# A read of the third gather back, ahead of each gather of an image's first six chunks

## The chip, the core and the metric

The kernel runs on one core of a Trainium2 chip. A core has five engines with their own instruction streams: TensorE (PE, matrix products and transposes), VectorE (DVE), ScalarE (ACT), GpSimd (POOL) and SyncE (SP, which here only starts transfers). Sixteen DMA engines move data between the chip's memory (HBM) and the core's own (SBUF). The metric is the device time of one launch in microseconds. The three runs of the kernel before gave 4634.28, 4643.66 and 4647.31 us, so the median is 4643.66 us.

## What is computed

The input is eight images of 256 channels and 64 x 64 pixels, all in f32. Two layers follow each other, each adding to its input. The first is a local attention of 3 x 3 pixels with a generated convolution kernel. The second, which the change is about, is a deformable 3 x 3 convolution: from the normed image a small convolution finds, for each pixel and each of nine taps, where to sample; four neighbouring pixels are read there, weighted, summed, and multiplied with the convolution's weights.

```python
# layer 0: group norm, 3x3 local attention, projection
x = x + _L0_conv_ref(_gn(x), w_qkv, w_kg, b_kg, alpha, beta, w_proj)
# layer 1: group norm, modulated deformable 3x3 convolution
x = x + _L1_conv_ref(_gn(x), w_off, b_off, w)
...
# in layer 1, with y0, x0, ly, lx from the offsets, for 9 taps and 64x64 pixels:
v = samp(y0, x0) * (1 - ly) * (1 - lx) + samp(y0, x0 + 1) * (1 - ly) * lx \
  + samp(y0 + 1, x0) * ly * (1 - lx) + samp(y0 + 1, x0 + 1) * ly * lx
return jnp.einsum('bckhw,ock->bohw', v * mask, w)
```

## The kernel before

**Two halves side by side.** An image is worked in eight chunks of 512 pixels. The "front" is the whole first layer and the preparation of the second: attention, norm, a table of the normed image in HBM, and the sampling places (`idx`) and weights (`wt`). The other half is the deformable convolution itself. While image b is convolved, the front of image b + 1 runs: `fronts()` is a generator that does one step at a time, and the main loop takes a step after each half slot. The last image is convolved without any front beside it. All four compute engines run their instructions in the order in which this program writes them down.

**The convolution.** A slot is one tap of one chunk: 72 slots an image, four blocks of 128 pixels in each, so 288 blocks an image and 2304 in all. A block goes through these lines:

- `gather` (line 1037): GpSimd issues an indirect DMA that reads, for each of 128 pixels, 4 KB from the table (all four corners, 256 channels each) into a buffer `g` of 128 x 1024 f32, 512 KB. There are ten such buffers (`GATHERS = 10`).
- `scale` (line 1053): ACT writes the first corner, times its weight, to `s`.
- `sum_corners` (line 1061): DVE adds the other three corners, each with its weight; three instructions a block, six in a row for a pair of blocks.
- `transposes` (line 1091): TensorE turns the four blocks' `s`; ACT copies the result to `vt` (line 1094).
- `product` (line 1116): TensorE multiplies with the weights, eight matmuls a slot, into `po`.

**What runs how far ahead.** At block i the loop scales blocks i + 8 and i + 9, sums blocks i + 6 and i + 7, then takes a step of the front, and then calls `gathers(i)`, which issues the gathers of blocks i + 16 and i + 17 (`LEAD = 16`). Their buffers are those of blocks i + 6 and i + 7, so they wait for the sums that were just put down. The DMAs of GpSimd go round eight semaphores ("lanes"): a gather waits for the landing of the gather eight before it, for DVE and for ACT.

**What else stands on GpSimd.** `gathers` first writes one element of a tile that TensorE is to have read (`holds`, the memset of line 1077), 223 times in all: the gathers behind it wait until TensorE is there. In the last image a memset of 128 x 160 (line 1082) follows each gather. In images 0 to 6 nothing stands between the two gathers of a pair.

**Other transfers.** SP starts loads of the next image's chunks, writes the table, stores the first layer's result (`kept`) and the output, and loads `r`, the first layer's result, back: 196 MB beside the gathers' 1208 MB. Loads of the next image stand mostly in the second half of an image's convolution.

The functions that the change touches, and what calls them:

Of the kernel before, what the change touches and what calls it, by code (L numbers as in the profile page):

```python
# [9 lines left out]
F32 = mybir.dt.float32  # L10
# [7 lines left out]
P = 128  # L18
# [7 lines left out]
NB = N // P  # L26
NC = H // R
KK = 9
# [17 lines left out]
BLOCKS = SLOTS * NB  # L46
# [3 lines left out]
LEAD = SUM_AHEAD + GATHERS  # L50
# [7 lines left out]
def preact_kernel(ctx: ExitStack, tc: tile.TileContext, a: dict, out: bass.AP):  # L58
# [17 lines left out]
    nc = tc.nc  # L76
# [3 lines left out]
    const = ctx.enter_context(tc.tile_pool(name="const", bufs=1))  # L80
# [74 lines left out]
    for i in range(min(2, B)):  # L155
# [7 lines left out]
        for o in range(H * WP, ENTRIES, P):  # L163
            n = min(P, ENTRIES - o)
# [862 lines left out]
    holds: list = []  # L1027
    rest = const.tile([P, 1], F32, name="rest")
    pause = const.tile([P, 160], F32, name="pause")

    def gather(i):
        if i >= B * BLOCKS:
            return
        b, n = divmod(i, BLOCKS)
        c, k, j = n // NB // KK, n // NB % KK, n % NB
        g = gp.tile([P, 4 * C], F32, tag="g", name=f"g_{i}")
        nc.gpsimd.indirect_dma_start(  # L1037
            out=g,
            out_offset=None,
            in_=tables[b % 2],  # L1040
            in_offset=bass.IndirectOffsetOnAxis(ap=found[b, c][0][:, j, k : k + 1], axis=1),
        )
        rows[i] = g
# [30 lines left out]
    def gathers(i):  # L1074

        if holds:
            nc.gpsimd.memset(holds.pop(), 0.0)
        last = i + LEAD >= (B - 1) * BLOCKS
        for n in range(2):
            gather(i + LEAD + n)  # L1080
            if last:
                nc.gpsimd.memset(pause, 0.0)
# [65 lines left out]
    with tc.manual_schedule(engines=ordered):  # L1148
# [24 lines left out]
        last = None  # L1173
        for n in range(B * SLOTS + 1):
            late, last = last, None
            if n > 0 and n % KK == 0:
                last = divmod(n // KK - 1, NC)
            for m in range(NT):
                if n < B * SLOTS:
                    if m == 0:  # L1180
                        transposes(*divmod(n, SLOTS))
                    if not last:
                        ahead(NB * n + 2 * m)
                if late and m == 0:
                    stored(*late)
                if n > 0:
                    product(*divmod(n - 1, SLOTS), m)
                if last:

                    finished(*last, m)  # L1190
                    ahead(NB * n + 2 * m)
                    if n == B * SLOTS:
                        stored(*last, slice(m, m + 1))

                h = NT * n + m + 1
                goal = h * STEPS + min(h, STEPS) * (STEPS_AHEAD - STEPS_FIRST)
                while (done - STEPS - STEPS_FIRST) * STEPS < goal:
                    state["quiet"] = next(steps, True)
                    done += 1
                if n < B * SLOTS:  # L1200
                    gathers(NB * n + 2 * m)
# [76 lines left out]
```

## Time and profile before

| | |
|---|---|
| median of three runs | 4643.66 us |
| the profiled execution | 4625.93 us |
| its span, first to last instruction | 4624.2 us |
| TensorE's granted clock, mean over the span | 0.992 |
| bytes moved | 1412.46 MB, 305 GB/s in the mean |
| gathers, all issued by GpSimd | 2304, 73.9% of the DMA engines' time |
| transfers started by SP and ACT | 11.7% of the DMA engines' time |

The profile is of one execution. "Busy" is the time in which an engine executes; time in which an instruction stands and waits is not in it. For each group of instructions the profile gives the busy time, the mean of one in ns, and the idle time of the engine just before them, with what ended that idle time: the engine or transfer whose signal came last. The chain of waits follows the work that ended last back through the span, and shares the span out among those that held it up. An indirect DMA shows as two things: the instruction on GpSimd, which writes the transfer's descriptors, and the transfer itself, whose packets and whose sixteen updates of its lane's semaphore are recorded too, not all of the updates.

Images 0 to 6 take about 555 us each. Within one, a chunk's 36 gathers take 65 to 70 us in chunks 0 to 5 and about 75 in chunk 6.

### The profile page before, as it was taken

Reading aid. Unit: us, or ns where it says so; the run is one execution under the profiler, and the core shown is the slowest. Engines: PE = TensorE matmul, PEld = TensorE weight load, DVE = VectorE, ACT = ScalarE, POOL = GpSimd, SP = SyncE. Lnnn points to the kernel's source line nnn. Section 1 sums busy time; section 2 is a strip of 40 time slices with the busy share of each in tenths; the row PEclk is TensorE's granted clock in tenths of the full one; section 3 lists DMA queues with packets and bytes.
Section 4 is the critical chain, followed back from the end, with each engine's and each line's share of the span. In section 5 each row is a group of like instructions: output and inputs, shape, how many; then the busy total and the mean of one; then the engine's idle time right before and its main releaser. Section 6 shows DMA issues by size and latency. Waiting matters only on the chain.

```text
span 4624.2 us, 77590 instructions
## 1 busy us (share of the span) xinstructions
PE 4486.9 (97%) x25344; PEld 2327.6 (50%) x25344; DVE 4132.8 (89%) x10183; ACT 2522.0 (55%) x5283; POOL 2685.1 (58%) x2840
## 2 busy tenths in 40 slices
PE   8989999999999999999999999999999999998888
PEld 4445555555545555455554555555555555543443
DVE  5669999999999999999998999999999999987887
ACT  3345556555565555655555555555556555554554
POOL 0035655566556655556655666555655656568887
PEclk9989999999999999999999999999999999999999
DMA  3078889988998888988899888998889988898998
GB/s 106 24 246 297 305 307 354 323 293 297 316 373 303 295 311 310 382 300 295 311 320 359 299 305 303 340 346 300 304 315 360 322 290 293 301 343 323 363 362 321
DMA packets 445761, 1412.46 MB, mean 305 GB/s; under 512 B 46430, under 2 KB 63070, under 8 KB 445228
## 3 DMA queue, kind: packets, MB, share of 16 engines
q0 software_dynamic: 331776, 1208.11, 73.9%
q1 hardware_dynamic: 111564, 196.04, 11.7%
q8 instruction: 199, 3.26, 0.3%
q10 hardware_dynamic: 2016, 3.36, 0.2%
q14 instruction: 206, 1.69, 0.1%
HBM read 1275.97 MB, written 131.36 MB: 304 GB/s over the span
## 4 chain that ended last, share of the span: by engine, by line
PE 84%; DMA 5%; DVE 5%; issue 2%; POOL 2%; ACT 2%; another core or an unknown queue 1%; SPq 0%; POOLq 0%; ACTq 0%; DVEq 0%
PE po L1116 37%; PE pt L1091 10%; PE psk L345 5%; PE proj L590 5%; PE psv L345 5%; PE psq L314 5%; PE om L817 4%; DMA g<-table,idx 3%; DVE s L1061 3%; PE av L577 3%; PE vk L559 2%; PE qk L388 2%; PE wk L536 2%; PE gen L431 1%; POOL g L1037 1%
## 5 line engine op out<-in xcount | busy, mean ns | idle before, releaser
L1037 POOL DMA_INDIRECT g<-table,idx x2304 | 2582.2, 1121 | 1702.6 <-issue 537.8
L1061 DVE SCALAR_TENSOR_TENSOR s<-g,wt,s 128x256 f32<-128x256 f32 x6912 | 2825.0, 477 | 162.2 <-ACT s L1053 124.3
L1116 PE MATMUL po<-vt,w_conv 128*128 128x512 f32 x4608 | 2192.0, 601 | 1.0 <-issue 1.0
L1116 PEld LDWEIGHTS po<-vt,w_conv 128*128 128x128 f32 x4608 | 810.8, 191 | 772.3 <-issue 763.2
L1053 ACT ACTIVATE s<-g,wt 128x256 f32<-128x256 f32 x2304 | 1058.6, 511 | 256.9 <-DMA g<-table,idx 187.5
L1094 ACT COPY vt<-pt 128x512 f32<-128x512 f32 x1152 | 617.3, 589 | 394.0 <-PE pt L1091 311.8
L1091 PE MATMUL pt<-ident,s 128*128 128x128 f32 x4608 | 648.0, 279 | 55.8 <-ACT vt L1094 21.6
L1091 PEld LDWEIGHTS pt<-ident,s 128*128 128x128 f32 x4608 | 522.2, 142 | 332.8 <-issue 173.6
L817 PE MATMUL om<-xn,w_off 128*32 128x512 f32 (+1 forms) x2560 | 273.8, 555 | 0.6 <-DVE xn L264 0.6
L345 PE MATMUL psv<-xn,w_qkvT 128*128 128x512 f32 (+1 forms) x576 | 248.9, 559 | 0.0
L345 PE MATMUL psk<-xn,w_qkvT 128*128 128x512 f32 (+1 forms) x576 | 246.9, 558 | 0.0
L314 PE MATMUL psq<-xn,w_qkvT 128*128 128x512 f32 x512 | 242.8, 605 | 3.9 <-issue 3.4
L590 PE MATMUL proj<-acc,w_projT 128*128 128x512 f32 x512 | 239.5, 593 | 0.7 <-ACT acc L584 0.7
L401 DVE TENSOR_TENSOR qk<-qk,near_k 128x400 f32<-128x400 f32 x256 | 134.7, 567 | 95.6 <-PE qk L388 55.9
L322 ACT COPY q<-psq 128x512 f32<-128x512 f32 x128 | 74.9, 585 | 235.8 <-PE psq L314 229.4
L584 ACT COPY acc<-av 128x512 f32<-128x512 f32 x128 | 74.8, 584 | 216.8 <-PE pt L1091 140.7
L356 ACT COPY k<-psk 128x512 f32<-128x512 f32 (+1 forms) x144 | 78.8, 551 | 201.8 <-PE psk L345 182.4
L577 PEld LDWEIGHTS av<-wk,vk 100*64 100x64 f32 x4096 | 132.2, 137 | 101.6 <-issue 49.7
L817 PEld LDWEIGHTS om<-xn,w_off 128*32 128x32 f32 x2560 | 75.6, 109 | 208.4 <-issue 201.1
L564 ACT COPY vk<-vk 100x512 f32<-100x512 f32 x256 | 139.1, 592 | 72.6 <-PE vk L559 62.3
L544 DVE TENSOR_TENSOR wk<-wk,near 100x512 f32<-100x512 f32 x256 | 158.6, 680 | 12.7 <-PE wk L536 12.7
L345 PEld LDWEIGHTS psk<-xn,w_qkvT 128*128 128x128 f32 x576 | 104.4, 190 | 122.6 <-issue 109.7
(104 smaller groups left out, 3440.3 us busy)
## 6 DMA issues: line engine op xcount, KB each, us to landing
table<-ts SPq DMA_DIRECT2D x128, 384.0 KB
g<-table,idx POOLq DMA_INDIRECT x2304
x<-in_x_dram SPq DMA_DIRECT2D x61, 512.0 KB
x<-x SPq DMA_DIRECT2D x56, 512.0 KB
r<-x SPq DMA_DIRECT2D x56, 512.0 KB
out_dram<-r SPq DMA_DIRECT2D x56, 512.0 KB
table<-ts SPq DMA_DIRECT2D x128, 128.0 KB
out_dram<-y SPq DMA_DIRECT2D x7, 512.0 KB
```

The source lines that it names most:

```text
L314: nc.tensor.matmul(ps, w_qkvT[:, ct, m * P : (m + 1) * P], window(self.xn, ct, 4), start=(ct == 0), stop=(ct == NT - 1),)
L345: nc.tensor.matmul(ps[:, : (hi - lo) * W], w_qkvT[:, ct, o : o + P], self.xn[:, ct, lo:hi, 1 : W + 1], start=(ct == 0), stop=(ct == NT - 1),)
L544: nc.vector.tensor_mul(wk.rearrange("p (t n) -> p t n", n=T * T), ps[:NK].rearrange("p (t n) -> p t n", n=T * T), near.unsqueeze(1).to_bro ...
L577: nc.tensor.matmul(av[64 * h : 64 * h + 64, g, t * T * T : (t + 1) * T * T], self.vk[:, t, o : o + 64], self.wk[2 * g + h][:, i * n + t * ...
L590: nc.tensor.matmul(ps, w_projT[:, ct, m * P : (m + 1) * P], self.acc[:, ct].rearrange("p (t y x) -> p y t x", y=T, x=T), start=(ct == 0), ...
L817: nc.tensor.matmul(self.ps[32 * g : 32 * g + 32, cols], w_off[:, ct, k, :], window(self.xn, ct, k)[:, ys], start=(n < 4), stop=(tail >= 0),)
L1037: nc.gpsimd.indirect_dma_start(out=g, out_offset=None, in_=tables[b % 2], in_offset=bass.IndirectOffsetOnAxis(ap=found[b, c][0][:, j, k : ...
L1053: nc.scalar.activation(s, g[:, 0:C], AF.Copy, scale=w[:, 0:1])
L1061: nc.vector.scalar_tensor_tensor(s, g[:, q * C : (q + 1) * C], w[:, q : q + 1], s, ALU.mult, ALU.add)
L1091: nc.tensor.transpose(pt[ct][:, j, :], s[:, ct * P : (ct + 1) * P], ident)
L1094: nc.scalar.copy(v[:, ct, :], pt[ct].rearrange("p b n -> p (b n)"))
L1116: nc.tensor.matmul(po[m], w_conv[:, ct, k, m * P : (m + 1) * P], v[:, ct, :], start=(k == 0 and ct == 0), stop=(b + 1 < B and k == KK - 1 ...
```

## The change

Ahead of each of the two gathers, GpSimd copies one element per partition (128 x 1) of the buffer of the gather that stands three ahead of it in the order of gathers into a new tile `landed`, which nothing reads. A copy must wait until the buffer that it reads has landed. It is done while `i % 288 < 216`, that is while the first six chunks of an image are convolved, and not once gathers of the last image are issued. Since gathers run 16 blocks ahead, these are the 17th to the 232nd gather of each of images 0 to 6: 216 x 7 = 1512 copies.

```diff
@@ -1027,6 +1027,7 @@
     holds: list = []
     rest = const.tile([P, 1], F32, name="rest")
     pause = const.tile([P, 160], F32, name="pause")
+    landed = const.tile([P, 1], F32, name="landed")
 
     def gather(i):
         if i >= B * BLOCKS:
@@ -1077,6 +1078,8 @@
             nc.gpsimd.memset(holds.pop(), 0.0)
         last = i + LEAD >= (B - 1) * BLOCKS
         for n in range(2):
+            if i % BLOCKS < (NC - 2) * KK * NB and not last:
+                nc.gpsimd.tensor_copy(landed, rows[i + LEAD + n - 3][:, 0:1])
             gather(i + LEAD + n)
             if last:
                 nc.gpsimd.memset(pause, 0.0)
```

In the program as built, each copy waits for the lane of the gather three before and for GpSimd's own earlier copy, and the gather behind it waits for DVE and ACT alone: its wait for the gather eight before is no longer written, since the copy's covers it. On the other four engines the instructions stand in the same order as before.

## The prediction

> **What bounds the kernel now.** First the page's busy line and its chain: TensorE is busy nearly all the span and carries 84% of the chain that ended last. The gathers hold 3%; of the 187.5 us that ACT's scaling (line 1053) waits for gathers, 140.6 lie in the last image (from 4200 us on) and 12.9 in the seven stretches below.
>
> ```profile
> span 4624.2 us, 77590 instructions
> PE 4486.9 (97%) x25344; PEld 2327.6 (50%) x25344; DVE 4132.8 (89%) x10183; ACT 2522.0 (55%) x5283; POOL 2685.1 (58%) x2840
> PE 84%; DMA 5%; DVE 5%; issue 2%; POOL 2%; ACT 2%; another core or an unknown queue 1%; SPq 0%; POOLq 0%; ACTq 0%; DVEq 0%
> L1037 POOL DMA_INDIRECT g<-table,idx x2304 | 2582.2, 1121 | 1702.6 <-issue 537.8
> ```
>
> Next the busy time by stage, for the seven stretches in which the gathers issue that the change touches (the 17th to the 232nd of each of images 0 to 6). First column the stretch, then its length, then busy us of each engine, clock, DMA share and GB/s.
>
> ```profile
> 315.70:726.80 411.10, 409.18 (x2356) 218.06 (x2356) 387.21 (x928) 228.48 (x491) 246.11 (x246) 1.00 0.86 296
> 1984.90:2390.50 405.60, 403.80 (x2340) 215.30 (x2339) 380.16 (x913) 223.91 (x481) 244.93 (x246) 1.00 0.88 303
> sum 2847.50, PE 2834.11 PEld 1510.43 DVE 2667.88 ACT 1576.24 POOL 1712.61; mean PE 404.87 PEld 215.78 DVE 381.13 ACT 225.18 POOL 244.66
> ```
>
> TensorE is idle 2847.5 - 2834.1 = 13.4 us of these 2847.5. So nothing in these stretches can be made faster by more than 13 us (0.3%); what can change is that TensorE is made to wait. The 1512 gathers there come one per 2847.5 / 1512 = 1.883 us. That is the pace to hold.
>
> **What the change adds.** In the built order each of the 1512 gathers gets a copy of 128x1 ahead of it on GpSimd, which waits for the semaphore of the gather three before. GpSimd runs in order, so gather n can't start until gather n-3 has landed: at most three are under way. Nothing is removed but the gather's own wait for the landing of the gather eight before, which the copy's wait covers. Nothing is moved: the order on the other engines is unchanged. Queued behind a waiting copy on GpSimd are its gather, the next pair with its copies, and the one-element holds of line 1077; who waits for them is ACT's scaling (line 1053), behind it DVE's sums (1061), the transposes (1091), TensorE.
>
> **Does the limit bind?** The trace records the semaphore updates of the eight gather lanes. Of the 1512 gathers, 741 have at least 14 of their 16 updates on record. From the start of the gather's instruction to its last update these take 6.05 us in the mean (5.04 at the tenth percentile, 7.39 at the ninetieth). A gather three ahead is still on its way when the next one starts in 52% of the cases. So the limit binds at once in half of all issues, and the question is whether three in flight can keep the pace: that is so while a turn of the ring (gather n-3 starts, to gather n starts) is under 3 x 1.883 = 5.65 us.
>
> **A turn of the ring, step by step.**
>
> 1. Start of a gather to its last semaphore update, when it isn't crowded. 316 gathers that start under 1.3 us after the one before (the second of a pair) take 6.43 us in the mean. The 57 that start 2.0 to 2.4 us after the one before and over 3.6 us after the one before that, which is the spacing that the limit would make, take 5.45. The 24 that start over 4 us after the one before take 4.65. I take 5.45; the ends are 4.65 and 6.05.
> 2. Update to the next engine's start: ACT's scalings that waited for a gather start 0.08 us after its last update.
> 3. The copy. The trace has no copy on GpSimd; the nearest row is the one-element memset of line 1077, 0.10 us. But a copy also reads, and a gather's instruction, which reads its indices, shows what that may cost: 0.93 us at its shortest and 1.12 in the mean of these 1512, so 0.18 us of waiting. I take 0.10 + 0.18 = 0.28; the ends are 0.10 (never held up) and 0.10 + 2.86 (six back-to-back sums of 0.477 us waited out each time).
> 4. Copy to the gather's start. The timeline of GpSimd shows it where a hold stood waiting: in the median 0.63 us pass from its end to the gather, as against 0.30 between two gathers.
>
> ```profile
> L1061 DVE SCALAR_TENSOR_TENSOR s<-g,wt,s x6912: 411/477/540, 294.1 to 4610.7; 128x256 f32<-128x256 f32 x198
> L1037 POOL DMA_INDIRECT g<-table,idx x2304: 932/940/5495, 289.3 to 4602.8; - x192
> ```
>
> ```profile
> L1077 POOL MEMSET vk<- x112: 98/98/118, 359.2 to 4046.0; 100x1 f32 x112
> ```
>
> ```profile
> 1171.51 2.29 POOL L1037 DMA_INDIRECT g<-table,idx  x1 [0.30 <-issue]
> 1174.52 0.10 POOL L1077 MEMSET q<- 128x1 f32 x1 [0.72 <-PE qk L388]
> 1175.25 0.95 POOL L1037 DMA_INDIRECT g<-table,idx  x1 [0.63 <-ACT s L1053]
> 1176.50 1.05 POOL L1037 DMA_INDIRECT g<-table,idx  x1 [0.30 <-DVE qk L401]
> 1177.85 1.68 POOL L1037 DMA_INDIRECT g<-table,idx  x1 [0.30 <-issue]
> ```
>
> In the first two fences read shortest/median/longest ns; in the third, start, length, and in brackets the idle time before. The 0.63 behind the memset is the engine's way from a released wait to a gather, and it stands in the ring each time the copy has waited.
>
> Turn: 5.45 + 0.08 + 0.28 + 0.63 = 6.44 us, so 2.15 us per gather against 1.883. The limit doesn't hold the pace.
>
> **The sum.** 1512 x 2.147 = 3246 us instead of 2847.5: 399 more. Off it goes the lead that each image starts with: a gather lands 5.4 us (median) ahead of the scaling that reads it, and that is eaten up before anyone waits: 7 x 5.4 = 38 us. Net 361 us. Chunks 6 and 7, and the last image, have no copies and keep their time; the lead refills there. GpSimd's own work isn't the bound: 1.12 + 0.28 + 0.63 = 2.03 us per gather, under 2.15. DVE loses at most 1512 x 0.1 us to the copies, beside 12% more time. Once TensorE waits a tenth of the time its clock might fall; in the last image it is busy 369.3 of 424 us at 0.98, so I put that at nothing. The profiled execution took 4625.93 us with a span of 4624.2: 4625.93 + 361 = 4987, **4990 us**. That execution is 18 us under the median of the three runs, 4643.66; I keep its scale, and the difference is inside the range.
>
> **Two rules weighed.** The trace gives 5.45 us from a gather's start to its landing. The Trainium skill, "DMA: Bandwidth & Descriptors", section "Anatomy of one DMA — SWDGE (gpsimd) path", fits such a DMA as about 2.0 us plus bytes over 436 GB/s. For 512 KB that is an estimate of 3.2 us; with the instruction's 1.12 ahead of it 4.3, the turn would be 5.3 us, 1.77 per gather, and the change would cost nothing. No gather here was timed with the DMA engines idle; they are 86 to 88% busy, so I follow the row. For the copy, "SBUF — State Buffer", section "Who interferes with whom", says that a DVE instruction with two SBUF inputs and a GpSimd instruction that reads SBUF shut each other out, but one that only writes goes free. So the memset's even 98 ns would say nothing of the copy. By the rule a copy waits for the sum then running, 0.48 us at most; that is 0.16 us per gather in the ring at the very worst, and no run here shows it yet.
>
> **The rivals.**
>
> *The limit costs nothing* (not slower). Spread evenly, the gathers no longer queue behind each other and land sooner. It decides at a landing time of 5.65 - 0.08 - 0.28 - 0.63 = 4.66 us, which the 24 loneliest gathers just have (4.65). Then the turn is 5.64 us and TensorE keeps its pace: 4626 to 4645 us, and at best 13 us less. For it: half the traffic's bunching goes away. Against it: those 24 have nothing else in flight, and the 254 that start at least 2 us after the one before, and 3.6 after the one before that, still take 5.43.
>
> *Each copy is held up by DVE* (more than forecast). DVE is busy 2667.9 of 2847.5 us there, most of it sums in runs of six. If a copy waits out half a run, 1.43 us, instead of 0.18, the turn is 7.69 us, 2.56 per gather, 1029 - 38 = 991 us more: 5617. Against it: gathers get through with 0.18 in the mean.
>
> *The change doesn't hold anything back*, since a gather needn't wait for a copy that it doesn't use. Against it: both are on one engine, in order, and a hold shows the gather behind it starting after it. Time 4626 to 4645.
>
> **How the numbers follow.** A tenth of a microsecond in the turn is 50 us. My terms leave about 0.5 us either way (5.45 against 4.65 or 6.05; 0.28 against 0.10 or a whole sum), so 250 us: 4740 to 5250 holds the forecast with 0.77. The limit that costs nothing has 0.09, the copy that holds nothing 0.02, the held-up copies (over 5250) 0.12. Faster or slower by 0.3% (14 us) is about what a measurement of this kernel can tell from no change. Faster 0.03, same 0.06, slower 0.91.
>
> **What would show it.** Right: ACT's scaling (line 1053) waits for gathers by hundreds of us in these stretches instead of 12.9; the stretches last about 460 us each instead of 405; a copy's gap is put down to the gather's landing; gap before a gather about 0.6. Step 1 is wrong if gathers land in under 4.9 us or over 6; step 3 if copies take far from 0.28 us. The whole is wrong if TensorE's idle time in the stretches stays near 2 us each.

## The result and the profile after

The changed kernel takes 5087.44 us (median of four runs, 5079.05 to 5099.94) against 4641.88 us for the kernel before beside it: the ratio is 1.0962, with an interval of 1.0948 to 1.0976. Forecast were 4990 us and a range of 4740 to 5250. The profiled execution took 5099.94 us.

The page of the kernel after, with the lines that answer to those of before; first the busy line, then the chain by engine and by line, then groups (busy, mean ns of one | idle before, and what ended it).

```profile
span 5097.9 us, 80537 instructions
PE 4654.3 (91%) x25344; PEld 2412.2 (47%) x25344; DVE 4152.4 (81%) x10183; ACT 2549.3 (50%) x5283; POOL 3163.1 (62%) x4352
...
PE 35%; DMA 29%; DVE 17%; ACT 7%; issue 6%; POOL 4%; another core or an unknown queue 1%; SPq 0%; ACTq 0%; POOLq 0%; DVEq 0%
...
L1054 ACT ACTIVATE s<-g,wt 128x256 f32<-128x256 f32 x2304 | 1118.2, 511 | 1407.6 <-DMA g<-table,idx 1241.0
L1082 POOL COPY landed<-g 128x1 f32<-128x1 f32 x1512 | 522.0, 345 | 586.8 <-DMA g<-table,idx 559.8
```

TensorE's share of the chain fell from 84 to 35%, and that of the transfers rose from 5 to 29%. ACT's scalings, now line 1054, waited 1241.0 us for gathers where it had been 187.5. The last line is the change itself: 1512 copies, and 559.8 of the 586.8 us of idle time before them were ended by a gather's landing (681 times).

In the seven stretches with copies alone the scalings waited 1094.6 us for gathers, where it had been 12.9. The fourth of them, before and after (total us, times, longest):

```profile
ACT s L1053 <- DMA g<-table,idx: 1.6, 1, 1.6
```

```profile
ACT s L1054 <- DMA g<-table,idx: 162.8, 116, 4.1
```

The busy time by stage, in the stretches in which the copies stand (the 17th to the 232nd gather of each image, as before):

```profile
322.20:787.80 465.60, 420.89 (x2328) 222.05 (x2327) 381.62 (x907) 227.82 (x479) 309.00 (x461) 0.97 0.80 262
2170.30:2640.90 470.60, 428.87 (x2345) 228.24 (x2344) 385.28 (x916) 230.02 (x484) 306.38 (x462) 0.96 0.81 261
sum 3306.80, PE 2995.66 PEld 1585.13 DVE 2693.01 ACT 1609.99 POOL 2180.76; mean PE 427.95 PEld 226.45 DVE 384.72 ACT 230.00 POOL 311.54
```

The seven stretches grew from 2847.5 to 3306.8 us, so 459 of the 474 us between the two spans lie there. TensorE is now idle 311 us in them, not 13. A gather comes every 2.187 us instead of 1.883.

GpSimd's timeline in one of them (start, length, idle time before and who ended it) shows the ring:

```profile
2309.89 0.18 POOL L1082 COPY landed<-g 128x1 f32<-128x1 f32 x1 [0.69 <-DMA g<-table,idx]
2310.60 0.97 POOL L1038 DMA_INDIRECT g<-table,idx  x1 [0.54 <-ACT s L1054]
2311.91 0.18 POOL L1082 COPY landed<-g 128x1 f32<-128x1 f32 x1 [0.34 <-DMA g<-table,idx]
2312.62 0.97 POOL L1038 DMA_INDIRECT g<-table,idx  x1 [0.53 <-issue]
...
2324.53 2.31 POOL L1082 COPY landed<-g 128x1 f32<-128x1 f32 x1 [0.81 <-DMA g<-table,idx]
```

These copies stand until a gather has landed; about 0.53 us after the copy's end the next gather starts, whatever name stands in its bracket. About half of the 1512 copies stand like this: 817 had over 0.05 us of idle time ahead of them. At the others the gather had landed while GpSimd was still busy with the instruction before. The last line is a copy that took 2.31 us itself.

### The profile page after: what moved, and what is told of

It reads as the page before. It is cut to its first block, busy times and chain, and to the rows that moved or that the text cites. A ratio compares the mean times of both kernels' runs of the same rounds, so it can differ in the third digit from the quotient of the medians.

```text
span 5097.9 us, 80537 instructions
## 1 busy us (share of the span) xinstructions
PE 4654.3 (91%) x25344; PEld 2412.2 (47%) x25344; DVE 4152.4 (81%) x10183; ACT 2549.3 (50%) x5283; POOL 3163.1 (62%) x4352
## 4 chain that ended last, share of the span: by engine, by line
PE 35%; DMA 29%; DVE 17%; ACT 7%; issue 6%; POOL 4%; another core or an unknown queue 1%; SPq 0%; ACTq 0%; POOLq 0%; DVEq 0%
DMA g<-table,idx 27%; PE po L1119 14%; DVE s L1062 12%; PE pt L1094 4%; PE om L817 4%; ACT s L1054 3%; POOL g L1038 3%; PE psv L345 2%; PE proj L590 2%; PE psq L314 2%; PE psk L345 2%; DMA x<-in_x_dram 1%; PE av L577 1%; ACT vt L1097 1%
## 5 line engine op out<-in xcount | busy, mean ns | idle before, releaser
L1038 POOL DMA_INDIRECT g<-table,idx x2304 | 2541.4, 1103 | 1301.3 <-issue 469.9
L1119 PE MATMUL po<-vt,w_conv 128*128 128x512 f32 x4608 | 2262.4, 617 | 0.0
L1054 ACT ACTIVATE s<-g,wt 128x256 f32<-128x256 f32 x2304 | 1118.2, 511 | 1407.6 <-DMA g<-table,idx 1241.0
L1119 PEld LDWEIGHTS po<-vt,w_conv 128*128 128x128 f32 x4608 | 838.3, 198 | 805.2 <-issue 796.1
L1082 POOL COPY landed<-g 128x1 f32<-128x1 f32 x1512 | 522.0, 345 | 586.8 <-DMA g<-table,idx 559.8
L1094 PE MATMUL pt<-ident,s 128*128 128x128 f32 x4608 | 678.6, 288 | 94.3 <-ACT vt L1097 47.9
L1094 PEld LDWEIGHTS pt<-ident,s 128*128 128x128 f32 x4608 | 548.8, 147 | 374.4 <-issue 183.8
L577 PE MATMUL av<-wk,vk 100*64 100x64 f32 x4096 | 168.6, 237 | 90.7 <-ACT vk L564 89.3
L388 PE MATMUL qk<-k,q 64*64 64x100 f32 x4096 | 140.9, 262 | 80.1 <-ACT k L356 64.1
L564 ACT COPY vk<-vk 100x512 f32<-100x512 f32 x256 | 137.3, 584 | 150.7 <-POOL vk L1078 108.7
L388 PEld LDWEIGHTS qk<-k,q 64*64 64x64 f32 x4096 | 106.1, 137 | 158.5 <-ACT k L356 73.9
L584 ACT COPY acc<-av 128x512 f32<-128x512 f32 x128 | 74.7, 583 | 210.1 <-POOL q L1078 154.3
```

Of the source, the lines that this page charges most:

```text
L577: nc.tensor.matmul(av[64 * h : 64 * h + 64, g, t * T * T : (t + 1) * T * T], self.vk[:, t, o : o + 64], self.wk[2 * g + h][:, i * n + t * ...
L1038: nc.gpsimd.indirect_dma_start(out=g, out_offset=None, in_=tables[b % 2], in_offset=bass.IndirectOffsetOnAxis(ap=found[b, c][0][:, j, k : ...
L1054: nc.scalar.activation(s, g[:, 0:C], AF.Copy, scale=w[:, 0:1])
L1082: nc.gpsimd.tensor_copy(landed, rows[i + LEAD + n - 3][:, 0:1])
L1094: nc.tensor.transpose(pt[ct][:, j, :], s[:, ct * P : (ct + 1) * P], ident)
L1119: nc.tensor.matmul(po[m], w_conv[:, ct, k, m * P : (m + 1) * P], v[:, ct, :], start=(k == 0 and ct == 0), stop=(b + 1 < B and k == KK - 1 ...
```

## The experiments

The theory to be tested: in the stretches a gather comes every max(1.883 us, turn / number allowed in flight), and a turn is landing time + wait to copy + copy + copy to gather. The rivals were that the copies cost by themselves, and that the holds, which now came late, made part of the loss. The kernel before took 4600 to 4649 us in the different runs beside these, so ratios are compared, and absolute times only within a run. "Landing time" is from the start of a gather's instruction to its last recorded semaphore update, mean of the gathers with at least 14 of 16 updates on record; "pace" is the summed length of the seven stretches over 1512.

**The same copies, four ahead, and six ahead.**

```diff
-                nc.gpsimd.tensor_copy(landed, rows[i + LEAD + n - 3][:, 0:1])
+                nc.gpsimd.tensor_copy(landed, rows[i + LEAD + n - 4][:, 0:1])   # first kernel
+                nc.gpsimd.tensor_copy(landed, rows[i + LEAD + n - 6][:, 0:1])   # second kernel
```

> The copy reads the gather four ahead instead of three; the same 1512 copies. Ring theory: a turn of about 6.0 (landing, one more in flight) + 0.13 + 0.35 + 0.53 = 7.0 us, shared by four, is 1.75 us per gather, under the 1.883 that TensorE asks for: 4640 to 4665 us. Rival, the copies cost by themselves (GpSimd's time, 1.10 + 0.35 + 0.53 + 0.16 = 2.14 us per gather, whatever they wait for): 4980 to 5090 us, as with three.

> The copy reads the gather six ahead, which has nearly always landed; the same 1512 copies. Ring theory: 4635 to 4660 us, and the copies wait for landings by under 20 us in all. Rival, the copies cost by themselves: 4980 to 5090 us. In between (4700 to 4900): both have a share, and this run gives the copies' share.

Four ahead: 1.0063 (1.0046 to 1.008). Six ahead: 0.9995 (0.9985 to 1.0004). The groups of the copies, with four first and then with six:

```profile
L1082 POOL COPY landed<-g 128x1 f32<-128x1 f32 x1512 | 650.7, 430 | 182.9 <-DMA g<-table,idx 168.3 <-DVE s L1062 0.7 <-POOL q L1078 0.4
```

```profile
L1082 POOL COPY landed<-g 128x1 f32<-128x1 f32 x1512 | 660.7, 437 | 9.6 <-POOL q L1078 0.3
```

With six the copies keep GpSimd busy for 660.7 us, more than with three, and cost nothing: no landing ends a wait of theirs. So a copy that has nothing to wait for costs nothing, and the first rival falls. With four they still waited 168.3 us and the pace was 1.907, against 1.864 with six on the same chip. The mean turn, 6.0 + 0.13 + 0.43 + 0.46 = 7.0, would allow 1.75. The likely reason, not tested by itself, is that the limit touches local bursts even where it is under the mean pace, which a sum over means, as in the expectation, doesn't see; its cost there is 0.6%.

**Without the holds,** in the changed kernel and in the kernel before.

```diff
-            nc.gpsimd.memset(holds.pop(), 0.0)
+            holds.pop()
```

> The changed kernel without the 223 one-element holds on GpSimd (pacing only). ACT waited 263 us for holds that came late. Ring theory: those waits are the ring's own lag seen at another place, and ACT would wait for gathers instead: 5060 to 5095 us. Rival, late holds made the 100 us beyond the forecast: 4970 to 5010 us.

> The kernel before without the holds, as the control of the run above. Both theories: within 20 us of the kernel before, 4625 to 4665 us; what it differs by is taken off the run above.

The changed kernel without holds: 1.0956 (1.0937 to 1.0975); the kernel before without them: 0.9995 (0.9986 to 1.0005). ACT's longest waits, of the changed kernel and then of the same without holds (total us, times, longest):

```profile
ACT s L1054 <- DMA g<-table,idx: 1241.0, 899, 5.6
ACT acc L584 <- POOL q L1078: 154.3, 41, 5.6
...
ACT vk L564 <- POOL vk L1078: 108.7, 47, 4.0
```

```profile
ACT s L1054 <- DMA g<-table,idx: 1619.2, 1239, 7.4
```

The 263 us that ACT stood waiting for late holds (154.3 for `acc`, 108.7 for `vk`) are not a loss of their own. Without the holds it waits 378 us longer for gathers, 1619.2 us, and the loss is the same. This is what a wait on a chain looks like when another wait on the same chain is taken away. The second rival falls.

**Two ahead.** The edit is `- 2` for `- 3`.

> The copy reads the gather two ahead. Ring theory: a turn of about 5.2 (landing, one fewer in flight) + 0.13 + 0.35 + 0.53 = 6.2 us, shared by two, 3.1 us per gather: 1512 x (3.1 - 1.88) = 1840 us more, ratio 1.36 to 1.43. Rival, each copy that must wait adds a fixed part of its own (as many copies, a few more of them waiting): ratio 1.10 to 1.20.

1.2961 (1.293 to 1.2992), between the two forecasts: more than the rival's fixed part per copy gives, less than the ring was given. The trace shows where the size was off: with two in flight a gather lands in 4.69 us, not 5.2. With the other parts as measured here the turn is 4.69 + 0.13 + 0.26 + 0.50 = 5.58 us, half of it 2.79, and the pace is 2.787. The ring holds; the landing time is what moves.

```profile
L1082 POOL COPY landed<-g 128x1 f32<-128x1 f32 x1512 | 392.0, 259 | 1439.7 <-DMA g<-table,idx 1432.9 <-issue 2.7
```

Nearly every copy now waits for a landing, 1432.9 us in all.

**A copy only ahead of the first of each pair.**

```diff
-            if i % BLOCKS < (NC - 2) * KK * NB and not last:
+            if n == 0 and i % BLOCKS < (NC - 2) * KK * NB and not last:
```

> Three ahead, but a copy only ahead of the first gather of each pair: 756 copies. Ring theory: the first of a pair starts after the second of the pair two before has landed (6.2, crowded) + 0.13 + 0.35 + 0.53, and that one started 1.26 after its own first: 8.5 us for four gathers, 2.12 us per gather, 1512 x 0.24 - 38 = 320 us more, ratio 1.06 to 1.08. Rival, the cost goes with the number of copies: half of 9.6%, ratio 1.045 to 1.05.

1.06 (1.0571 to 1.0628), pace 2.085 against the forecast 2.12. Half of the copies keep 62% of the loss. The ring says so, since one wait per pair still ties four gathers to one landing; a price per copy doesn't.

**A write in place of the read.**

```diff
-                nc.gpsimd.tensor_copy(landed, rows[i + LEAD + n - 3][:, 0:1])
+                nc.gpsimd.memset(rows[i + LEAD + n - 3][:, 0:1], 0.0)
```

> The copy is replaced by a one-element memset into the buffer of the gather three ahead: the same wait, but GpSimd writes and doesn't read. It spoils the first channel of one corner in those blocks. If reading is what makes the copy long (0.35 us in the mean, 0.18 at its shortest), the memset takes about 0.11, the turn is 0.24 us shorter, and 1512 x 0.08 = 120 us come back: ratio 1.065 to 1.075. If not, 1.09 to 1.10.

1.0752 (1.0719 to 1.0785), pace 2.124.

```profile
L1082 POOL MEMSET g<- 128x1 f32 x1512 | 159.8, 106 | 646.9 <-DMA g<-table,idx 554.8 <-DVE s L1062 59.3 <-issue 6.3
```

The memset takes 106 ns in the mean, 124 at the 99th percentile; the copy 345, from 182 to 3623. So about a fifth of the loss was the copy's reading, by way of the turn: the memset is 0.24 us shorter than the copy, but the landing time rose to 5.64 us and the median way to the gather, where there was a wait, to 0.60, so 0.063 us per gather came back, not 0.08. The share is not exact, since the memset brings waits of its own: it stood 59.3 us for DVE, and most of ACT's scalings that waited now waited for it (1022.2 us) and not for the gather itself. That a write goes free and a read doesn't agrees with the Trainium skill, "SBUF — State Buffer", section "Who interferes with whom". The same page's "Summary: rules for kernel authors" has the second one to issue blocked until the first finishes. DVE's timeline of the changed kernel beside the copy of 2.31 us shown above (2324.53 to 2326.84) differs in that:

```profile
2323.99 1.66 DVE L1062 SCALAR_TENSOR_TENSOR s<-g,wt,s 128x256 f32<-128x256 f32 x4
2325.57 1.21 DVE L1140 TENSOR_TENSOR r<-y,r 128x1024 f32<-128x1024 f32 x1
2326.71 1.64 DVE L412 TENSOR_REDUCE by<-qk 128x480 f32<-128x1440 f32 x1
```

The copy stood through the rest of four sums and an addition, all with two inputs, back to back, and ended just after DVE had gone on to an instruction with one input. The longest copy, 3623 ns, stood through six sums and such an addition. So a read can be passed over by a whole run of them: 36 of the 1512 copies took over 1.5 us, and all 36 ended 0.01 to 0.13 us after DVE had begun an instruction other than these sums and additions.

**Half the bytes.**

```diff
-            out=g,
+            out=g[:, 0 : 2 * C],
...
-                    s, g[:, q * C : (q + 1) * C], w[:, q : q + 1], s, ALU.mult, ALU.add
+                    s, g[:, q % 2 * C : (q % 2 + 1) * C], w[:, q : q + 1], s, ALU.mult, ALU.add
```

> The changed kernel, but each gather reads 2 KB for each pixel instead of 4 and the sums use the first two corners twice: two corners are left out, all else is the same. If the landing time of a gather is in good part its bytes, it falls from 5.5 to about 4.8 us, the turn to 5.8, the pace to 1.93: ratio 1.005 to 1.03. Rival, the landing time is a fixed latency that bytes don't change: ratio 1.08 to 1.10.

The kernel leaves out two of the four corners. Its ratio is 0.9988 (0.9976 to 0.9999). The landing time fell further than forecast, to 3.74 us; the turn is then, with the other parts as with four ahead, 3.74 + 0.13 + 0.43 + 0.46 = 4.8 us, 1.59 per gather, and the limit hardly ever binds (70.7 us of the copies' waits). Its busy time by stage, two of the stretches:

```profile
881.50:1289.10 407.60, 406.39 (x2345) 216.19 (x2344) 380.94 (x915) 225.50 (x484) 332.57 (x462) 1.00 0.56 164
1990.50:2401.50 411.00, 407.90 (x2342) 217.01 (x2341) 382.14 (x916) 224.12 (x482) 329.12 (x461) 1.00 0.56 163
```

The three ahead that cost 9.6% cost nothing here: the DMA engines are busy 56% of the time (second last column) and the gathers are back early enough. That shows the landing time as the term that decides.

**The same again, and in three images only.**

```diff
-            if i % BLOCKS < (NC - 2) * KK * NB and not last:
+            if i % BLOCKS < (NC - 2) * KK * NB and i < 3 * BLOCKS:   # second kernel; the first is unaltered
```

> The changed kernel once more, unaltered, for the last image, which has no copies but took 446.0 us (from its 17th gather) instead of 423.5 in the first pair of profiles, at a granted clock of 0.92 instead of 0.98. Ring theory alone: ratio 1.09 to 1.10, and nothing said of the last image. If the change itself lengthens the last image: 440 to 450 us again. If it is the chip or the execution: about 421 to 430.

> The copies, three ahead, only in images 0 to 2: 648 of them. Ring theory: each limited image costs 1512 x (2.19 - 1.88) / 7 = 66 us less 2 to 4 that its tail gives back, so 186 to 195 us, ratio 1.040 to 1.043, and images 3 to 6 take their old time. Rival, a cost that starts once (a lower clock that stays, a lead that is lost and doesn't come back): images 3 to 6 stay longer too, ratio over 1.05. The last image, four images after the last copy, should be at 421 to 430 us if a limited image right before it is what lengthened it.

Again: 1.0968 (1.0939 to 1.0997), the stretches 3306.9 us once more, the last image 422.2 us. So the copies need not lengthen the last image, which had taken 446.0 us instead of 423.5 in the first pair of profiles. What did lengthen it there stays open: this run was on another chip, and on a third one it took 433 us with two ahead, 440 with the first of each pair and 443 with the memset, at a granted clock of 0.94 to 0.95. Three images: 1.0431 (1.0402 to 1.046). Image 2 and image 3 of that run, one with and one without copies:

```profile
1551.90:2022.80 470.90, 429.32 (x2348) 227.26 (x2347) 385.98 (x917) 230.15 (x485) 313.88 (x461) 0.96 0.81 261
2166.20:2572.40 406.20, 404.23 (x2341) 215.64 (x2340) 380.32 (x913) 224.03 (x481) 238.92 (x246) 1.00 0.88 302
```

As soon as the copies are gone the stretch has its old length and TensorE its old clock. Nothing is carried over.

## Why the prediction was right

The cause, the direction and the place were as forecast: three gathers in flight can't keep the pace, and the loss lies in the seven stretches. Term by term, forecast and then measured in the changed kernel:

| term | forecast | measured |
|---|---|---|
| landing time, us | 5.45 | 5.54 (5.50 in the repeated run) |
| landing to copy, where the copy waited | 0.08 | 0.13 |
| copy | 0.28 | 0.345 |
| copy to gather, where the copy had waited | 0.63 | 0.53 |
| turn | 6.44 | 6.54 by these, 6.56 by the pace |
| pace per gather | 2.147 | 2.187 |
| more in the stretches | 399 | 459 |
| given back by the lead | 38 | 14.5 |

The agreement of 6.54 with 6.56 is in part luck, since the 0.13 and the 0.53 are medians of the 817 copies that waited. What doesn't depend on that choice: the two ways together are 6.56 - 5.54 - 0.345 = 0.68 us in the mean, against 0.71 forecast. The copy's 0.28 was put together as 0.10 and 0.18 of waiting; the shortest copy took 0.18, and 0.16 in the mean came on top.

The time came out 97 us over the forecast of 4990, and 100 over the unrounded 4987. This has three parts. The turn was 0.12 us longer, which is 60 us: landing and copy were a little low, the way to the gather a little high. The lead gave back less: the seven tails without copies shrank from 1037.4 to 1022.9 us, 14.5 and not 38, which is 24 us. And the forecast was left on the scale of a profiled execution that ran 16 us under the median of its kernel. 60 + 24 + 16 = 100. In the profiled pair itself 474 us were added: 459 in the stretches less 14.5 in the tails, and, with no term in the forecast, 22.5 in the last image and 6.5 ahead of the first stretch. Without these two it is 445, as much as the medians grew (446).

The landing time of 5.45, a fair guess, was read from the trace of before, by picking the gathers that happened to have the spacing that the limit would make. The row for all gathers, 6.05, would have given a pace of 2.35 us and, by the same sum, 663 us of loss where 446 were measured; the row of the 24 that the prediction called loneliest, 4.65, no loss at all.

The rival in which nothing is lost asked for a landing time under 4.66 us with three in flight. It was 5.54; but 4.69 was reached with two, so the way the rival thought was right and the load too high for it. The prediction held against it that those 24 had nothing else in flight. The trace of before says otherwise: 23 of them started while the gather before was still on its way, and in all 24 the next one started, 1.2 us later, before they landed. The fit of the Trainium skill for such a DMA ("DMA: Bandwidth & Descriptors", section "Anatomy of one DMA — SWDGE (gpsimd) path") had given about 4.3 us with the instruction's own time for 512 KB. The half-byte run is the place to hold it against: an estimate of 2.0 + 0.6 us by the page and 1.1 by the trace for the instruction gives 3.7 us, and 3.74 was measured, at DMA engines 56% busy. At 80% and three in flight the estimate is 1.2 us short, and the measurement decides.

The rival in which every copy stands behind DVE was right in kind and small in size: 0.345 us, not 1.53.

What the prediction passed over: it named ACT's scaling as the one that would wait. ACT's writes of `vk` and `acc` wait as well, for holds that stand behind copies on GpSimd (263 us). The run without holds shows that this cost nothing more. It also put TensorE's clock at nothing. The clock did fall, to 0.96 in the stretches, and TensorE's busy time there rose by 162 us. GpSimd's own time shows that this didn't set the pace. Its 3306.9 us are 1643 of gathers' instructions, 520 of copies, 551 from a copy to its gather, 572 ahead of copies (550 of it ended by a landing) and 20 of the rest. The 551 are nearly all the fixed way of 0.53 us after a copy that had waited and 0.16 after one that hadn't (817 x 0.53 + 695 x 0.16 = 544). So GpSimd hardly waited for anything but landings, and without the 572 us its pace would be 1.81 us per gather, under the 1.883 asked for.

"Gap before a gather about 0.6" and "the stretches about 460 us" came out as 0.53 and 466 to 477.

## What to carry to other kernels

How many transfers may be in flight is a budget: needed are landing time over pace, here 6.0 / 1.883 = 3.2 (3.7 with the rest of the turn, 7.0 us), and the landing time has to be read under the load that the limit itself makes, to the last semaphore update and with the way from the released wait to the next start. Here a limit a little over that number cost 0.6%, one a little under it 9.6%, and the lead in the buffers gave back only 14.5 us. When a wait is added, it's the wait and not the instruction that is to be priced: 1512 copies that had nothing to wait for cost nothing, though they were busy for 661 us.

## What the runs showed of the hardware

- A gather's landing time rose with the number allowed under way: 4.69 us with two, 5.54 with three, 5.99 with four, 6.02 with six, 6.05 before, where ten buffers set the limit. With half the bytes and at most three in flight it was 3.74. The busy share of the DMA engines rose along with the number (about 65% with two, 80% with three, 87% with four and six), and no run tells the two apart.
- A one-element copy on GpSimd took 182 ns at its shortest, 345 in the mean and 3623 at its longest beside a busy DVE; a one-element memset in the same place 106 in the mean.
- From the last update of a gather to a waiting copy it took 0.125 us (median), and from the end of a copy that had waited to the next gather 0.53; where the copy had not waited, 0.16.
- TensorE's granted clock fell as it waited more: 1.00 in the stretches before, 0.95 to 0.97 with three in flight, 0.87 to 0.89 in the first two stretches with two. It came back to 1.00 in the next stretch without copies.
